# Placing small VectorE steps inside a matmul round, and pairing the context products of a two-layer graph network kernel

## The chip, the cores and the metric

The kernel runs on one core of one Trainium2 chip. The metric is device time in microseconds (us), from the first to the last instruction of the slowest core; here there is only one core. Three runs of the kernel before took 2916.56, 2917.6 and 2920.24 us, so the median is 2917.6 us. Engines are named as in the profile: PE (TensorE matmuls), PEld (TensorE weight loads), DVE (VectorE), ACT (ScalarE), POOL (GpSimd) and SP (SyncE, which here only issues transfers).

## The reference, cut to what matters

128 graphs with 64 nodes of 768 features pass through two layers; everything is fp32.

```
# layer 0, for each graph: h is 64 x 768, adj is 64 x 64
p    = softmax(h h^T / sqrt(768));  d = p * adj;  attn = d / (sum(d) + 1e-10)
ctx  = upper(attn) @ (h Wl^T + bl) + diag(attn) * (h Ws^T + bs) + lower(attn) @ (h Wr^T + br)
x    = layernorm(h + relu(layernorm(ctx) * gamma + beta))
# layer 1: 12 heads of 64 features
q, k, v = x Wq + bq, x Wk + bk, x Wv + bv
s    = q k^T / 8 + beta * adj, set to -9e15 where adj is 0
out  = layernorm(x + softmax(s) @ v)
```

The changed lines belong to layer 0: to the two products with Wl and Wr (the left and the right sides) and to the products of the attention matrix with them (the context).

## The kernel before, in words

**Blocks.** The 8192 tokens are cut into 16 blocks of 512 tokens (`NBLK`), each of four token tiles of 128 (`T`). In the steady state the loop `for n in range(NBLK)` works on layer 1 of block n and on layer 0 of block m = n + 1 at once, stage by stage: first the left and right sides of block m, then the self part of m, then the values of block n (with the context of m tucked in), then the query and key products of n for three groups of heads.

**Fast matrix products.** Large products use a seven-product scheme in place of eight (a Strassen-like scheme; `ORDER`, `ORDER2`). `seven` runs it on one level. `nested` (lines 425 to 501) runs it on two levels for the left and right sides of blocks 3 to 15: seven outer rounds i in the order 7, 1, 2, 6, 5, 4, 3, and in each of them seven inner products j. The inner products of two rounds are interleaved: after products 6, 5, 7 of round i come products 1 and 2 of the next round, and then 4 and 3 of round i. Below, 7(2) means inner product 7 of outer round 2. Products 1, 6, 7 and 4 of a round accumulate in one PSUM tile, X; product 2 writes a tile Y, and products 5 and 3 another. After products 1, 2, 6, 7, 4 and 3 the sum so far is read out of PSUM, plus a partner, into SBUF: this is an eviction (`middle`, `final`, `taken`, lines 439 to 458). Round 7 evicts most of X with ACT, the others evict with DVE at line 443. The next product that adds to the same PSUM tile has to come behind the eviction that reads it.

**Steps.** All other small work is kept in three queues, `first`, `urgent` and `lazy`, and a little of it is handed out by `step` behind each product (lines 137 to 156). An ordinary step lets DVE do one piece; a light step (`light=True`) issues no plain DVE piece and only takes pieces of other kinds, such as an ACT piece or a gap. In `sub` (lines 460 to 486) the call `step(len(done) > 8, j in (5, 1, 4))` makes the steps behind inner products 5, 1 and 4 light. So DVE pieces come behind 6, 7, 2 and 3. During the two-level stage these pieces are:

- of the layer-1 scores of an earlier block: an addition of the mask (line 860), a maximum (861), a subtraction (862), then 16 exponentials on ACT (853) and two transposes on DVE (857);
- of two weighted sums (`weighted`): four pieces each, a reciprocal (890) and four multiply-adds (894), which read PSUM tiles of the pool `ps_mm`.

**Context.** `context0` (lines 664 to 736) multiplies, for each of the four token tiles t, the transposed attention matrix with the left and right sides: four matmuls on 64 columns of the array each, into two PSUM tiles of `ps_mm` (a pool of four), behind them two DVE multiply-adds (line 684) and one ACT sum (687). These four `part`s are hung between the products of `values`, at places 1, 3, 5 and 7 of its 14 products; the steps that need all four sums come at place 9. In block 0 all four parts run in a row.

**Order.** Under `tc.manual_schedule()` the instructions of each engine stand in the order in which the code issues them. SP fetches the weights of the two-level stage (`wlr`, 63 pieces of 192 KB for each block, line 634) and all other weights into one pool of 19 buffers (`wst`).

Of the kernel before, what the change touches and what calls it, by code (L numbers as in the profile page):

```python
# [11 lines left out]
F32 = mybir.dt.float32  # L12
AF = mybir.ActivationFunctionType
ALU = mybir.AluOpType
# [3 lines left out]
P = 128  # L18
B, L, D = 128, 64, 768
# [3 lines left out]
HALF = D // 2  # L23
# [28 lines left out]
def gnn_two_layers(ctx: ExitStack, tc, x, adj, wl, bl, ws, bs, wr, br, gamma, beta,  # L52
                   wq, bq, wk, bk, wv, bv, abeta, out):
    nc = tc.nc
# [14 lines left out]
    ps_mm = ctx.enter_context(tc.tile_pool(name="ps_mm", bufs=4, space=PSUM))  # L69
# [51 lines left out]
    def later(key, *fs, queue=lazy):  # L121
        queue.extend((key, f) if callable(f) else (key, *f) for f in fs)
# [14 lines left out]
    def step(act_free=True, light=False):  # L137
        with tc.issue_after(recent["u"].ins) if recent.get("bound") else ExitStack():
            of_queues(act_free, light)
# [18 lines left out]
    def freed():  # L158

        while first:  # L160
            first.popleft()[1]()
# [12 lines left out]
    start = ExitStack()  # L174
# [250 lines left out]
    def nested(width, sums, load, multiply, view, C, bias0, bias1, hooks):  # L425

        X, Y, U, F, W = {}, {}, {}, {}, {}  # L430
        c11, c12, c21, c22 = C[0, 0], C[0, 1], C[1, 0], C[1, 1]
        out = {7: c22, 1: c21, 2: c11, 6: c21, 5: c12, 4: c21, 3: c12}
        old = {2: c21, 6: c21, 5: c21, 4: c21, 3: c12}
        done = []

        def part(i, q):
            return bias0(q[1]) if i == 1 else old[i][q] if i in old else None

        def taken(i, q, ps, dst, add):
            if add is None:  # L440
                nc.scalar.copy(dst, view(ps))
            else:
                nc.vector.tensor_tensor(dst, view(ps), add, ALU.add)  # L443

        def middle(i, q, ps, k):
            u = tmp.tile([P, HALF], F32, tag="u1" if k == 2 else "u0", name="u_deep")
            U[i, k] = view(u)
            taken(i, q, ps, U[i, k], part(i, q))
            if i == 5:
                nc.gpsimd.tensor_tensor(c21[q], c21[q], c22[q], ALU.add)  # L450

        def final(i, q, ps, add):
            taken(i, q, ps, out[i][q], add)
            if i == 5:
                if q == (1, 0):
                    nc.gpsimd.tensor_tensor(c21[q], c21[q], c22[q], ALU.add)
                nc.gpsimd.tensor_tensor(c12[q], c12[q], bias1(q[1]), ALU.add)
                nc.gpsimd.tensor_tensor(c22[q], c22[q], c12[q], ALU.add)

        def sub(i, j):  # L460
            for place in range(28):
                if place * 49 // 28 == len(done):
                    for f in hooks.get(place, ()):
                        f()
            done.append((i, j))
            if j == 1:
                X[i] = ps_st.tile([P, 512], F32, tag="X", name="ps_X")
            if j in (2, 5):
                Y[i] = ps_st.tile([P, 512], F32, tag="Y", name="ps_Y")
            ps = (X if j in (1, 6, 7, 4) else Y)[i][:, 0:width]  # L470
            multiply(F[i], W[i], j, ps)
            if j == 1:
                middle(i, (0, 0), ps, 1)
            elif j == 2:
                final(i, (0, 0), ps, U[i, 1])
            elif j == 6:
                middle(i, (0, 1), ps, 2)
            elif j == 7:
                middle(i, (1, 1), ps, 3)
                final(i, (1, 1), Y[i][:, 0:width], U[i, 3])  # L480
            elif j == 4:
                final(i, (1, 0), ps, part(i, (1, 0)))
            elif j == 3:
                final(i, (0, 1), ps, U[i, 2])

            step(len(done) > 8, j in (5, 1, 4))

        F[ORDER2[0]], W[ORDER2[0]] = sums(ORDER2[0]), load(ORDER2[0])
        sub(ORDER2[0], 1)
        sub(ORDER2[0], 2)  # L490
        for k, i in enumerate(ORDER2):
            after = ORDER2[k + 1] if k + 1 < len(ORDER2) else None
            if after:
                F[after], W[after] = sums(after), load(after)
            for j in (6, 5, 7):
                sub(i, j)
            if after:
                sub(after, 1)
                sub(after, 2)
            for j in (4, 3):  # L500
                sub(i, j)
# [162 lines left out]
    def context0(n):  # L664


        blk = blocks[n]
        xa, o, dg = blk["xa"], blk["x"], blk["dg"]
        by_act = n > 0
        if by_act:  # L670
            total, nm, var, std, rstd = (st.tile([P, T], F32, tag=f"c{k}", name=f"c{k}") for k in range(5))

        def unused():
            return l1s_p.tile([P, T * 4 * L], F32, tag="s", name="unused")[:, 0:D]

        def part(t):
            freed()
            for h in range(2):
                cols = slice(h * HALF, (h + 1) * HALF)
                ps = ps_mm.tile([P, 512], F32, tag="mm", name="ps_ctx")  # L680
                for g in range(2):
                    nc.tensor.matmul(ps[g * L : (g + 1) * L, 0:HALF], lhsT=blk["aT"][:, t, g * L : (g + 1) * L],  # L682
                                     rhs=blk["lr"][t][:, g, cols], start=True, stop=True)
                nc.vector.scalar_tensor_tensor(o[t][:, cols], o[t][:, cols], dg[:, t : t + 1], ps[:, 0:HALF],  # L684
                                               ALU.mult, ALU.add)
            if by_act:
                nc.scalar.activation(unused(), o[t], AF.Identity, accum_out=total[:, t : t + 1])  # L687
            elif t == T - 1:
                rest(moments(key, o, 1e-12))

        key = ("o", n)

        def squares():
            nc.vector.tensor_scalar(nm, total, -1.0 / D, None, ALU.mult)
            for t in range(T):
                nc.scalar.activation(unused(), o[t], AF.Square, bias=nm[:, t : t + 1], accum_out=var[:, t : t + 1])

        def roots():
            nc.vector.tensor_scalar(std, var, 1.0 / D, 1e-12, ALU.mult, ALU.add)
            nc.scalar.activation(std, std, AF.Sqrt)  # L700

        def inverse():
            nc.vector.reciprocal(rstd, std)
            rest([(nm[:, t : t + 1], rstd[:, t : t + 1]) for t in range(T)])

        def affine(t, mean, rstd):
            nc.vector.scalar_tensor_tensor(o[t], o[t], mean, affine_of["gamma"], ALU.add if by_act else ALU.subtract,
                                           ALU.mult)

        def affine2(t, mean, rstd):  # L710
            nc.vector.scalar_tensor_tensor(o[t], o[t], rstd, affine_of["beta"], ALU.mult, ALU.add)

        def residual(t):
            nc.vector.scalar_tensor_tensor(o[t], o[t], 0.0, xa[t], ALU.max, ALU.add)

        squared = 0 < n < NBLK - 1
        blk["x_d"] = x_d = tc.dram_tile([NTOK, D], F32, name=f"x1d_{n}") if squared else None

        def norm(t, mean, rstd):
            nc.vector.tensor_scalar(o[t], o[t], mean, rstd, ALU.subtract, ALU.mult)  # L720

        def stored():
            settle(key)
            for t in range(T):
                nc.gpsimd.dma_start(out=x_d[t * P : (t + 1) * P, :], in_=o[t])

        blk["stored"] = stored

        def rest(factors):
            for t, mr in enumerate(factors):  # L730
                fs = partial(affine, t, *mr), partial(affine2, t, *mr), partial(residual, t)
                later(key, *(fs if by_act else (fs[0], lambda fs=fs: (fs[1](), fs[2]()))))
            fs = [partial(norm, t, *mr) for t, mr in enumerate(moments(key, o, 1e-5))]
            later(key, *(fs if by_act else (lambda: (fs[0](), fs[1]()), lambda: (fs[2](), fs[3]()))))

        return [partial(part, t) for t in range(T)], (squares, roots, inverse)


# [283 lines left out]
    for n in range(NBLK):  # L1022
        m, p = n + 1, n - 1
        left, right, own, val = {}, {}, {}, {}
        qk = [{}, {}, {}]

        def at(hooks, place, f, *args):
            hooks.setdefault(place, []).append(partial(f, *args))
# [27 lines left out]
        if not last:  # L1056
            if n > 0:
# [9 lines left out]
                when, place = (left, 10) if n > 1 else (right, 2)  # L1067
# [45 lines left out]
                        at(own, 1 + t, f)  # L1113
                self_part(m, None, own)
            tiles, normal = context0(m)
            for t, f in enumerate(tiles):
                at(val, 1 + 2 * t, f)
            for hooks, place, f in ((val, 9, normal[0]), (val, 13, normal[1]), (qk[0], 1, normal[2])):
                at(hooks, place, f)
            if m + 1 < NBLK:  # L1120
# [163 lines left out]
```

## Time and profile before

| what | value |
|---|---|
| median of three runs | 2917.6 us |
| span of the profiled execution | 2916.3 us |
| median less that span | 1.3 us |
| PE busy | 2872.5 us, 98% of the span |
| DVE, ACT, POOL busy | 68%, 38%, 25% |
| granted TensorE clock, mean | 0.998 |
| PE instructions | 17578 (each fp32 matmul shows as two) |

The profile's busy time of PE counts the modelled end of each matmul, so that a short stall partly hides in it; stalls are read better from the distance between two starts. In the stages spoken of here an undisturbed instruction on 128 x 384 elements starts 0.3225 us after the one before it (24 of them take 7.74 us in the chain of waits), so that a product of one matmul takes 0.645 us (1, 6, 7) and one of two takes 1.29 us (2, 5, 4, 3).

In a timeline each line gives the start in us, the duration in us, the engine, the source line, the operation, what is written and read, the shapes and the number of merged instructions; the square bracket at its end is the idle time of the engine ahead of it and what ended it.

### The profile page before, as it was taken

The numbers are of one execution on the slowest core, as the hardware profiler recorded it, in microseconds if no ns is written. First come the engines' busy times: TensorE is split into PE (matmuls) and PEld (weight loads), VectorE is DVE, ScalarE is ACT, GpSimd is POOL, SyncE is SP. The second block draws the span as 40 slices with busy tenths as digits, with TensorE's granted clock in tenths as the row PEclk, the third lists the DMA queues.
The fourth block names the chain that finished last, engine by engine and source line by source line (L and its number), as shares of the span: only waits on it lengthen the run. The fifth ranks groups of instructions, "written<-read, shape, count | busy, mean of one in ns | idle before, by whom it ended". The sixth has DMA issues, their size and how long they took to land.

```text
span 2916.3 us, 49872 instructions
## 1 busy us (share of the span) xinstructions
PE 2872.5 (98%) x17578; PEld 1932.9 (66%) x17578; DVE 1974.3 (68%) x3973; ACT 1122.4 (38%) x2107; POOL 732.4 (25%) x879
## 2 busy tenths in 40 slices
PE   9999999999999999999999999999999999999997
PEld 5658567585665857658576675766757567585685
DVE  6678777676676766757667576766767667676655
ACT  0004224354243443434444344443434524344255
POOL 3133123213142140412405123051230512314110
PEclk9999999999999999999999999999999999999999
DMA  9788877859677595775958669486684956849443
GB/s 340 222 274 275 253 219 200 243 145 286 154 213 234 157 278 148 222 226 167 269 146 244 197 181 268 136 272 173 186 260 138 284 162 196 247 140 289 138 127 99
DMA packets 440662, 613.18 MB, mean 210 GB/s; under 512 B 53584, under 2 KB 416720, under 8 KB 440416
## 3 DMA queue, kind: packets, MB, share of 16 engines
q1 hardware_dynamic: 362960, 495.93, 56.1%
q10 hardware_dynamic: 60848, 44.05, 8.0%
q0 software_dynamic: 16608, 70.01, 6.7%
q8 instruction: 143, 2.34, 0.3%
q14 instruction: 103, 0.84, 0.1%
HBM read 539.43 MB, written 77.27 MB: 211 GB/s over the span
## 4 chain that ended last, share of the span: by engine, by line
PE 96%; POOL 2%; issue 1%; DVE 1%; ACT 0%; DMA 0%; POOLq 0%; SPq 0%; ACTq 0%
PE ps_X L389 38%; PE ps_Y L389 28%; PE ps_Y L643 11%; PE ps_X L643 10%; PE ps_ctx L682 3%; PE sc L833 2%; PE ps_y L884 2%; PE u L532 2%; POOL q L342 1%; POOL q L341 0%; PE ps_x L291 0%; POOL q L343 0%; ACT eT L853 0%; DMA xa<-in_x_dram 0%; DVE u_deep L443 0%
## 5 line engine op out<-in xcount | busy, mean ns | idle before, releaser
L389 PE MATMUL ps_X<-xT,wqk 128*128 128x256 f32 x1728 | 391.9, 380 | 0.6 <-ACT uqk L801 0.6
L853 ACT ACTIVATE eT<-s 32x256 f32<-32x256 f32 x768 | 317.8, 414 | 171.6 <-DVE s L862 161.6
L389 PEld LDWEIGHTS ps_X<-xT,wqk 128*128 128x128 f32 x1728 | 327.0, 190 | 52.9 <-ACT k L807 4.6
L322 POOL TENSOR_TENSOR S<-hT 128x768 f32<-128x768 f32 x16 | 29.0, 1810 | 1133.6 <-PE ps_Y L389 1102.1
L389 PE MATMUL ps_Y<-S,wqk 128*128 128x256 f32 x1152 | 264.3, 379 | 0.0
L687 ACT ACTIVATE unused<-o 128x768 f32<-128x768 f32 x60 | 50.6, 844 | 499.6 <-DVE o L684 305.3
L389 PEld LDWEIGHTS ps_Y<-S,wqk 128*128 128x128 f32 x1152 | 218.9, 190 | 29.8
L443 DVE TENSOR_TENSOR lr<-ps_Y,u_deep 128x384 f32<-128x384 f32 x273 | 151.6, 555 | 96.8 <-PE ps_Y L643 71.0
L643 PE MATMUL ps_Y<-wlr,q 128*128 128x384 f32 x546 | 208.5, 491 | 0.0
L801 ACT ACTIVATE uqk<-ps_X,bq 128x256 f32<-128x256 f32 x144 | 68.3, 474 | 333.1 <-PE ps_X L389 332.4
L389 PE MATMUL ps_X<-wv,xT 128*128 128x384 f32 x576 | 195.5, 489 | 0.0
L389 PE MATMUL ps_X<-ws,hT 128*128 128x384 f32 x540 | 179.2, 486 | 0.0
L809 DVE TENSOR_TENSOR q<-ps_Y,uqk 128x256 f32<-128x256 f32 x144 | 61.0, 424 | 169.7 <-PE ps_Y L389 97.4
L643 PE MATMUL ps_X<-wlr,q 128*128 128x384 f32 x364 | 152.0, 499 | 16.8 <-POOL q L342 5.9
L389 PEld LDWEIGHTS ps_X<-wv,xT 128*128 128x128 f32 x576 | 108.0, 190 | 80.4 <-issue 8.4
L894 DVE SCALAR_TENSOR_TENSOR o<-ps_y,rz,o 128x64 f32<-128x64 f32 x720 | 154.7, 277 | 6.4
L443 DVE TENSOR_TENSOR u_deep<-ps_X,lr 128x384 f32<-128x384 f32 x195 | 107.3, 551 | 68.3 <-PE ps_X L643 66.6
L389 PEld LDWEIGHTS ps_X<-ws,hT 128*128 128x128 f32 x540 | 102.5, 190 | 71.4
L643 PEld LDWEIGHTS ps_Y<-wlr,q 128*128 128x128 f32 x546 | 101.6, 190 | 67.2
L420 DVE TENSOR_TENSOR u<-ps_X,bv 128x384 f32<-128x384 f32 x96 | 53.4, 556 | 130.9 <-PE ps_X L389 130.9
L389 PE MATMUL ps_X<-S,wqk 128*128 128x256 f32 x576 | 138.3, 385 | 0.0
L389 PE MATMUL ps_Y<-xT,wqk 128*128 128x256 f32 x576 | 135.6, 385 | 0.0
(258 smaller groups left out, 5467.2 us busy)
## 6 DMA issues: line engine op xcount, KB each, us to landing
wlr<-lr_d SPq DMA_DIRECT2D x819, 192.0 KB, 3.4
wqk<-qk_d SPq DMA_DIRECT2D x672, 192.0 KB, 2.4
wv<-d_v SPq DMA_DIRECT2D x192, 192.0 KB, 2.9
ws<-d_s SPq DMA_DIRECT2D x180, 192.0 KB, 5.7
wv<-in_L_gnn_Wv_dram SPq DMA_DIRECT2D x144, 192.0 KB, 4.1
ws<-in_L_gnn_W_self_dram SPq DMA_DIRECT2D x135, 192.0 KB, 5.4
xa<-in_x_dram SPq DMA_DIRECT2D x64, 384.0 KB, 4.9
sq<-in_x_dram ACTq DMA_DIRECT2D x56, 384.0 KB, 7.8
```

The costliest lines, as they stand in the source:

```text
L389: nc.tensor.matmul(ps, lhsT=a, rhs=b, start=(c == 0 and i in (1, 2, 5)), stop=(c == len(fs) - 1), skip_group_check=True)
L420: recent["u"] = evicted[nm] = nc.vector.tensor_tensor(u, ps, bias[nm][:, b * HALF : (b + 1) * HALF], ALU.add)
L443: nc.vector.tensor_tensor(dst, view(ps), add, ALU.add)
L532: nc.tensor.matmul(u[g * L : (g + 1) * L, t, :], lhsT=xT[:, c, tok], rhs=xT[:, c, tok], start=(c == 0), stop=(c == KC - 1))
L643: nc.tensor.matmul(ps, lhsT=a, rhs=b, start=(k == 0 and j in (1, 2, 5)), stop=(k == len(fs) - 1), skip_group_check=True)
L682: nc.tensor.matmul(ps[g * L : (g + 1) * L, 0:HALF], lhsT=blk["aT"][:, t, g * L : (g + 1) * L], rhs=blk["lr"][t][:, g, cols], start=True, s ...
L801: nc.scalar.activation(u, ps, AF.Identity, bias=bias["qk"[j]][:, c : c + 1])
L809: nc.vector.tensor_tensor(dst, ps, part, ALU.add)
L833: nc.tensor.matmul(sc[r][g * L : (g + 1) * L, t, c, :], lhsT=q[rows, c, tok], rhs=k[rows, c, tok], start=True, stop=True)
L853: nc.scalar.activation(e[to[0], :, to[1]], pairs[rows, :, cols], AF.Exp)
L884: nc.tensor.matmul(y[r, h][cols, t, c, :], lhsT=eT[rows, 2 * h + t, c, cols], rhs=v[rows, 2 * h + t, g, hg + c * HC, :], start=True, stop= ...
L894: nc.vector.scalar_tensor_tensor(res[:, r, c, hg, :], ps[:, t, c, 0:HD], rz[:, t, c : c + 1], res[:, r, c, hg, :], ALU.mult, ALU.add)
```

## The change

There are two edits. First, in the two-level stage the steps behind inner products 5, 1 and 3 are light, in place of 5, 1 and 4: the fourth DVE piece of a round comes behind product 4 and no longer behind product 3. Second, the context products of two token tiles are issued as one group, ahead of the first of their two `part`s, into all four tiles of the pool; and the four parts move from places 1, 3, 5, 7 to places 1, 2, 5, 6.

```diff
-            step(len(done) > 8, j in (5, 1, 4))
+            step(len(done) > 8, j in (5, 1, 3))
...
+        banks = {}
+
+        def multiplied(ts):
+            freed()
+            for t in ts:
+                for h in range(2):
+                    ps = banks[t, h] = ps_mm.tile([P, 512], F32, tag="mm", name="ps_ctx")
+                    for g in range(2):
+                        nc.tensor.matmul(ps[g * L : (g + 1) * L, 0:HALF], lhsT=blk["aT"][:, t, g * L : (g + 1) * L],
+                                         rhs=blk["lr"][t][:, g, h * HALF : (h + 1) * HALF], start=True, stop=True)
+
         def part(t):
-            freed()
+            if t % 2 == 0:
+                multiplied((t, t + 1))
             for h in range(2):
                 cols = slice(h * HALF, (h + 1) * HALF)
-                ps = ps_mm.tile([P, 512], F32, tag="mm", name="ps_ctx")
-                for g in range(2):
-                    nc.tensor.matmul(ps[g * L : (g + 1) * L, 0:HALF], lhsT=blk["aT"][:, t, g * L : (g + 1) * L],
-                                     rhs=blk["lr"][t][:, g, cols], start=True, stop=True)
-                nc.vector.scalar_tensor_tensor(o[t][:, cols], o[t][:, cols], dg[:, t : t + 1], ps[:, 0:HALF],
-                                               ALU.mult, ALU.add)
+                nc.vector.scalar_tensor_tensor(o[t][:, cols], o[t][:, cols], dg[:, t : t + 1],
+                                               banks.pop((t, h))[:, 0:HALF], ALU.mult, ALU.add)
...
             tiles, normal = context0(m)
-            for t, f in enumerate(tiles):
-                at(val, 1 + 2 * t, f)
+            for place, f in zip((1, 2, 5, 6), tiles):
+                at(val, place, f)
```

## The prediction

> **What bounds the kernel now.** I read the page first, then PE's waits, then the timelines of one two-level stage (block 5, 652 to 709 us) and of the values stage behind it. The page says that PE is the bound everywhere:
>
> ```profile
> PE 2872.5 (98%) x17578; PEld 1932.9 (66%) x17578; DVE 1974.3 (68%) x3973; ACT 1122.4 (38%) x2107; POOL 732.4 (25%) x879
> PE 96%; POOL 2%; issue 1%; DVE 1%; ACT 0%; DMA 0%; POOLq 0%; SPq 0%; ACTq 0%
> ```
>
> So only what makes PE faster counts. PE's waits (us in total, times, longest) show where it loses time: line 643, the two-level stage.
>
> ```profile
> PE ps_X L643 <- POOL q L342: 5.9, 13, 0.5
> PE ps_X L643 <- issue: 5.6, 29, 0.2
> PE ps_X L643 <- POOL q L344: 3.1, 13, 0.2
> ```
>
> The counts are 13, 13 and 29: the same few waits in each of 13 stages. The releasers named are not the true ones, as the timeline shows. PE first, from 3(7)'s end to 1(2):
>
> ```profile
> 664.16 0.81 PE L643 MATMUL ps_X<-wlr,q 128*128 128x384 f32 x2
> 664.81 0.81 PE L643 MATMUL ps_Y<-wlr,q 128*128 128x384 f32 x2
> 665.46 0.81 PE L643 MATMUL ps_Y<-wlr,hT 128*128 128x384 f32 x2
> 666.47 0.88 PE L643 MATMUL ps_X<-wlr,q 128*128 128x384 f32 x2 [0.21 <-issue]
> 667.19 0.81 PE L643 MATMUL ps_X<-wlr,hT 128*128 128x384 f32 x2
> ```
>
> These are 6(1), 5(1) in two lines, 7(1) and 1(2). 7(1) should start at 664.81 + 1.29 = 666.10 and starts at 666.47: 0.37 us late. DVE at the same time:
>
> ```profile
> 664.37 0.56 DVE L443 TENSOR_TENSOR lr<-ps_Y,u_deep 128x384 f32<-128x384 f32 x1 [1.35 <-PE ps_Y L643]
> 664.84 0.17 DVE L890 RECIPROCAL rz<-ps_y 128x4 f32<-128x4 f32 x1
> 665.05 0.86 DVE L894 SCALAR_TENSOR_TENSOR o<-ps_y,rz,o 128x64 f32<-128x64 f32 x4
> 665.82 0.55 DVE L443 TENSOR_TENSOR u_deep<-ps_X,bias_lr 128x384 f32<-128x384 f32 x1
> ```
>
> The first line evicts 3(7); then comes the small piece behind product 3, 0.98 us; only then the eviction of 6(1), which could have begun at 664.81 + 0.2. Product 7 adds to the tile that this eviction reads, and starts 0.65 us after its start. That is the true releaser. Around 7(2) the piece is the subtraction:
>
> ```profile
> 672.48 1.21 DVE L862 TENSOR_TENSOR s<-s,mx 128x1024 f32<-128x1024 f32 x1
> 673.61 0.55 DVE L443 TENSOR_TENSOR u_deep<-ps_X,lr 128x384 f32<-128x384 f32 x1
> ...
> 674.26 0.88 PE L643 MATMUL ps_X<-wlr,q 128*128 128x384 f32 x2 [0.46 <-POOL q L342]
> ```
>
> (673.61 to 674.26 is 0.65 again.) In the values stage, the second place where PE loses:
>
> ```profile
> 736.16 2.10 PE L389 MATMUL ps_X<-wv,xT 128*128 128x384 f32 x6
> 738.19 1.51 PE L682 MATMUL ps_ctx<-lr,aT 128*64 128x384 f32 x8
> 739.63 2.20 PE L389 MATMUL ps_X<-wv,xT 128*128 128x384 f32 x6
> 741.67 2.10 PE L389 MATMUL ps_Y<-wv,xT 128*128 128x384 f32 x6
> 743.70 1.51 PE L682 MATMUL ps_ctx<-lr,aT 128*64 128x384 f32 x8
> ```
>
> From one context group to the next is 743.70 - 738.19 = 5.51 us. The twelve ordinary instructions are worth 12 x 0.3225 = 3.87. Block 0, where all context products stand in one group, takes 5.31 us for 32 instructions, and 5.31 - 1.44 (the group of 8 here) over the 24 more is 0.161 each, so eight are worth 1.29. The remaining 0.35 us belongs to each group: some 0.10 ahead of it, 0.15 in it, 0.10 in the first matmul behind it.
>
> **What the Trainium skill says.** PSUM — Partial Sum Buffer, section "PSUM bank collisions raise a hardware error": two engines must not be on one bank's quadrant at once and software has to guard it by semaphore; so 7 cannot overlap the eviction of 6. The trace agrees: 0.65 us from start to start, twice. The same page, "Engine vs sequencer instructions": VectorE's queue is strictly first in, first out, so an eviction cannot pass a small piece; the DVE lines above agree. TensorEngine Tiling (Array Packing), "Key Properties": changing the tiling mode drains the array. The 0.35 us on every change from 128 to 64 columns and back agrees in kind. Perfetto Trace Analysis, "Optimization Strategy": the same gap repeating on the engine that should be saturated may mean too few buffers; here the trace shows late evictions instead.
>
> **Part 1, the moved step.** It removes no instruction; it moves one DVE piece per round ahead of the eviction of 3. No transfer of SP or POOL changes its place. On ACT, the exponentials now stand ahead of all four `sq<-x1d` loads instead of around the first.
>
> What it removes: the piece behind product 3 delays four products 7 of each stage. From starts: 7(1) 0.37; 7(2) 674.26 against 672.35 + 1.29 = 0.62; 7(6), behind a transpose, 681.83 against 680.14 + 1.29 = 0.40; 7(5) 690.66 against 689.00 + 1.29 = 0.37. The sum is 1.76. Each also stretches the product behind the stall from 0.645 to 0.72 (666.47 to 667.19), four times 0.075 = 0.30. Together 2.06 us a stage, 26.8 us in 13 stages. Other waits (6(7) on ACT, 4(3) on DVE) stay.
>
> What comes back: I walk DVE through the new order with these rows: eviction 0.47 to the next start, 0.6 to 0.65 where the next needs its result, weighted piece 0.98, eviction possible 0.2 after its product's end.
> - Round 7. The queue's contents shift too: the subtraction (1.13) now comes behind 4(7), from 663.1 to 664.2, while DVE used to wait (idle 1.35). Eviction of 3(7) at 664.37 as before, of 6(1) at 665.01, so 7(1) starts at 666.10: no stall.
> - Round 1. The four weighted pieces come behind 6, 7, 2(2) and 4(1). 7(1) evicted at 666.95 and 667.55, piece to 669.0, evictions of 1(2) and 2(2) at 669.0 and 669.64, piece to 671.09, eviction of 4(1) to 671.56, piece to 672.54, of 3(1) to 673.01, of 6(2) at 673.01. 7(2) can start at 673.66, and 5(2) ends at 673.20: a stall of 0.46, plus 0.075. DVE has a backlog here, and no place would hide it.
> - Round 2. The transposes come behind 6(2) and 7(2), nothing behind 4(2): no stall at 7(6).
> - Round 6. A piece behind 2(5) and one behind 4(6). With the PE times of this walk: 4(6) evicted 686.27 to 686.74, piece to 687.72, 3(6) to 688.19, 6(5) at 688.19, so 7(5) is free at 688.84, ahead of 689.14: no stall, by 0.30.
>
> So 0.53 us a stage remains and 2.06 - 0.53 = 1.53 goes: 19.9 us in 13 stages. The moved piece costs nothing otherwise because the eviction of 3 has no early reader on PE: the next product that adds to that tile is a full round away. Bounds: 0.53 more (26.8) if no backlog stall is left; half of 19.9, 10 us, if 7(5) and one more go on stalling.
>
> **Part 2, the pairs.** Matmuls, adds and sums are the same in number. In 15 blocks, four groups become two, and 2 x 0.35 = 0.70 us goes: 10.5 us. The moved adds (two of 0.6 us for tiles 1 and 3) come earlier, into a DVE that idles about 1.4 us ahead of nearly each eviction here; without that cover a late eviction would have to exceed a whole 1.94 us product. The group needs four `ps_mm` tiles at once: their last readers are the attention transpose's (706.84, a stage earlier) and, at place 5, the adds of tiles 0 and 1, issued three products (5.8 us) before. Bounds: 0, if changing tiles inside a group costs what the mode change does, against which block 0 speaks; 12.
>
> **Sum.** 19.9 + 10.5 = 30.4 us off the span, 2916.3 to 2885.9; the median runs stand 1.3 above the span: **2887.2 us**, 1.04% less.
>
> **Rivals.**
> 1. DVE's backlog only moves: product 7 goes on stalling in every loaded round, and part 1 brings 0 to 10 us. For it: round 1 shows exactly that. Against: before the evictions of 3(7), 3(2) and 3(6) DVE idles 1.35, 0.73 and 0.57 us, which is the room that the piece takes. It gives about 2897 to 2907 us.
> 2. No backlog stall is left, because DVE's pitch is a little shorter than in my walk (0.1 us in each of five places): 2880 us. Four pieces and seven evictions in one round (3.9 + 7 x 0.47 + 0.4 = 7.6 us against 7.1 of PE) speak against it.
> 3. Slower: on ACT the `sq<-x1d` loads are issued earlier, from about 671 us in place of 675, and could collide with `wlr`. A weight buffer comes round after 19 x 56.9 / 63 = 17 us; a `wlr` piece lands in 3.4 us (median), 8.6 at most. PE waits only from 17 us on; at 20 us, a loss of 2.8 a stage, the kernel is slower: about 2924 us. The DMA share argues against it: 0.73 from 666 to 673 us, 1.10 from 680 to 690, so the loads move to where there is room.
> 4. The edit does nothing: the order of the changed program's instructions does show the pieces ahead of 3's eviction and the groups of 16 on PE, so this is excluded but for 2% within 0.2%.
>
> **How the numbers follow.** My forecast 0.66, rival 1 0.17, rival 2 0.11, rival 3 0.04, no difference 0.02. Range 2878 to 2901: the forecast with its bounds, rival 2 and the better half of rival 1. About 0.2% (5.8 us) is what a measurement of this kernel can tell from no change: faster 0.94, same 0.02, slower 0.04.
>
> **What would show it.** PE's waits at line 643 fall from some 19.6 us to about 9; a single stall of about 0.46 a stage stays, at 7(2), besides those of 6(7) and 4(3); the stage of block 5 takes 55.4 us in place of 56.9. Context groups show 16 instructions in about 2.73 us, two for each block. Wrong would be: waits at 7(1), 7(6) or 7(5); a group of 16 that takes 2.9; PE waiting on `wlr`.

## The result, and the profile after

The changed kernel takes 2889.86 us (median of 4 runs, 2888.21 to 2891.61) against 2917.08 us for the kernel before (4 runs): a ratio of 0.9906, 95% interval 0.9893 to 0.9919. That is 27.2 us less; 30.4 were forecast (2887.2 us, range 2878 to 2901).

The page of the changed kernel, PE still the bound:

```profile
PE 2852.7 (99%) x17578; PEld 1940.3 (67%) x17578; DVE 1971.5 (68%) x3973; ACT 1121.9 (39%) x2107; POOL 717.5 (25%) x879
```

PE's waits at line 643 (us in total, times, longest). There were 78 before; 39 are left, three in each of the 13 stages, and their sum fell from 19.5 to 12.0 us:

```profile
PE ps_X L643 <- POOL q L344: 6.9, 13, 0.9
PE ps_X L643 <- DVE u_deep L443: 2.8, 13, 0.2
PE ps_X L643 <- issue: 2.3, 13, 0.2
```

The second and third are those of 4(3) and 6(7), which the change does not touch. The first is the one of 7(2).

The timelines are of the stage that the prediction calls that of block 5; the name is kept here, though it is the second of the 13 stages, so that in the count from 3 to 15 its block is number 4. DVE (start, duration, line, operation, what is written and read), from 4(7) to the eviction of 6(1): the subtraction, line 870 now, fills what was an idle gap, and the two evictions follow without a piece between them:

```profile
658.81 1.23 DVE L870 TENSOR_TENSOR s<-s,mx 128x1024 f32<-128x1024 f32 x1
660.13 0.56 DVE L443 TENSOR_TENSOR lr<-ps_Y,u_deep 128x384 f32<-128x384 f32 x1
660.77 0.56 DVE L443 TENSOR_TENSOR u_deep<-ps_X,bias_lr 128x384 f32<-128x384 f32 x1
```

PE at the same time: 5(1) in two lines, then 7(1) without a bracket, 1.29 us after the start of 5(1):

```profile
660.57 0.81 PE L643 MATMUL ps_Y<-wlr,q 128*128 128x384 f32 x2
661.22 0.81 PE L643 MATMUL ps_Y<-wlr,hT 128*128 128x384 f32 x2
661.86 0.81 PE L643 MATMUL ps_X<-wlr,q 128*128 128x384 f32 x2
```

DVE in the loaded round: the eviction of 4(1), the fourth weighted piece, the eviction of 3(1), that of 6(2):

```profile
666.87 0.55 DVE L443 TENSOR_TENSOR lr<-ps_X,bias_lr 128x384 f32<-128x384 f32 x1
667.33 0.17 DVE L898 RECIPROCAL rz<-ps_y 128x4 f32<-128x4 f32 x1
667.54 0.86 DVE L902 SCALAR_TENSOR_TENSOR o<-ps_y,rz,o 128x64 f32<-128x64 f32 x4
668.31 0.55 DVE L443 TENSOR_TENSOR lr<-ps_Y,u_deep 128x384 f32<-128x384 f32 x1
668.97 0.56 DVE L443 TENSOR_TENSOR u_deep<-ps_X,lr 128x384 f32<-128x384 f32 x1
```

and PE, where 7(2) is the one product 7 that still waits:

```profile
667.67 0.81 PE L643 MATMUL ps_Y<-wlr,q 128*128 128x384 f32 x2
668.31 0.81 PE L643 MATMUL ps_Y<-wlr,hT 128*128 128x384 f32 x2
669.62 0.88 PE L643 MATMUL ps_X<-wlr,q 128*128 128x384 f32 x2 [0.50 <-POOL q L344]
```

7(2) should start at 667.67 + 1.29 = 668.96; it is 0.66 us late, and 669.62 is again 0.65 after the start of the eviction that it needs (668.97). Last, the context on PE:

```profile
730.60 2.10 PE L389 MATMUL ps_X<-wv,xT 128*128 128x384 f32 x6
732.63 2.80 PE L684 MATMUL ps_ctx<-lr,aT 128*64 128x384 f32 x16
735.36 2.20 PE L389 MATMUL ps_X<-wv,xT 128*128 128x384 f32 x6
```

Sixteen instructions in 2.73 us (732.63 to 735.36), one entry and one exit for two tiles.

**Where the time went.** The two-level stage of block 5 took 56.93 us from its first product to the first of the self part (652.14 to 709.07); it now takes 55.61 (647.90 to 703.51): 1.32 us less. The 13 such stages together took 740.2 us and take 723.3, which is 16.9 less; 13 x 1.32 would be 17.2, but in one stage, which begins at 2243.3 us, 7(2) waits 0.87 us in place of 0.50 and the stage takes 55.98. The values stage took 33.65 us (736.16 to 769.81) and takes 32.95 (730.60 to 763.55): 0.70 us, in 15 blocks 10.5. These 27.4 us, and 0.7 us of PE's wait for the first load of `xa` (7.1 and 6.4 us in all, which varies from run to run), make 28.1 of the 28.2 us between the two spans (2916.3 and 2888.1); between the medians it is 27.2.

### The profile page after: what moved, and what is told of

Read it like the earlier page. It is cut to its first block, busy times and chain, and to the rows that moved or that the text cites. A ratio compares the mean times of both kernels' runs of the same rounds, so it can differ in the third digit from the quotient of the medians.

```text
span 2888.1 us, 49913 instructions
## 1 busy us (share of the span) xinstructions
PE 2852.7 (99%) x17578; PEld 1940.3 (67%) x17578; DVE 1971.5 (68%) x3973; ACT 1121.9 (39%) x2107; POOL 717.5 (25%) x879
## 4 chain that ended last, share of the span: by engine, by line
PE 97%; POOL 1%; issue 1%; DVE 1%; ACT 0%; DMA 0%; POOLq 0%; SPq 0%; ACTq 0%
PE ps_X L389 38%; PE ps_Y L389 28%; PE ps_Y L643 12%; PE ps_X L643 10%; PE ps_ctx L684 3%; PE sc L841 2%; PE ps_y L892 2%; PE u L532 2%; PE ps_x L291 0%; POOL q L343 0%; ACT eT L861 0%; DVE u_deep L443 0%; DMA xa<-in_x_dram 0%; POOL q L341 0%; POOL q L342 0%
## 5 line engine op out<-in xcount | busy, mean ns | idle before, releaser
L695 ACT ACTIVATE unused<-o 128x768 f32<-128x768 f32 x60 | 50.6, 843 | 478.7 <-DVE o L692 218.7
L948 ACT ACTIVATE unused<-o 128x768 f32<-128x768 f32 x60 | 50.6, 843 | 266.6 <-DVE o L902 165.6
```

## The experiments

The theory: DVE works through its queue in order, and a small piece ahead of the eviction of product 6 makes product 7 late; a change between 128 and 64 columns costs PE 0.35 us a group. The rivals are named with each run. All medians are compared with the kernel before, measured on the same chip (2917.16 us in the first four runs, 2917.49 in the last three). "Both edits" is the changed kernel, 2889.86 us where the kernel before took 2917.08.

**1. The moved step alone**

```diff
-            step(len(done) > 8, j in (5, 1, 4))
+            step(len(done) > 8, j in (5, 1, 3))
```

> Only the moved step, context groups as before. Theory (late evictions of product 6 behind a VectorE piece): the stage of block 5 takes 55.6 us as with both edits, against 56.9, so 13 x 1.32 = 17 us less than before: about 2900 us. Rival (the stage's gain comes from the changed context groups or from their earlier sums): no more than 3 us less, 2914 us or above.

Measured: 2899.91 us, ratio 0.9943 (0.993 to 0.9955). The stage of block 5 takes 55.60 us (650.02 to 705.62), as with both edits. The gain of this stage is that of the moved step and of nothing else.

**2. The pairs alone**

```diff
-            step(len(done) > 8, j in (5, 1, 3))
+            step(len(done) > 8, j in (5, 1, 4))
```

(an edit to the changed kernel)

> Only the paired context groups, steps as before. Theory (each entry into and exit from 64 columns costs 0.35 us in all): 15 x 0.70 = 10.5 us less than before, about 2906.6 us, with the waits at line 643 as before (19.5 us). Rival (the cost belongs to the matmuls or to changing PSUM tiles, not to the group): 0 to 3 us less, 2914 us or above.

Measured: 2907.73 us, ratio 0.9966 (0.9953 to 0.9978), so 9.4 us less. The values stage takes 32.95 us, as with both edits, and so brings 10.5 us in 15 blocks. The two parts add up: 17.25 and 9.4 are 26.7, both together gave 27.2. PE's waits at line 643 are those of before, 19.9 us in all:

```profile
PE ps_X L643 <- issue: 8.3, 39, 0.8
PE ps_X L643 <- POOL q L342: 5.5, 12, 0.5
...
PE ps_X L643 <- POOL q L344: 3.1, 13, 0.2
PE ps_X L643 <- DVE u_deep L443: 2.8, 13, 0.2
...
PE ps_X L643 <- POOL q L343: 0.2, 1, 0.2
```

**3. No piece behind 4 in the loaded round**

```diff
-            step(len(done) > 8, j in (5, 1, 3))
+            step(len(done) > 8, j in (5, 1, 3) or (i, j) == (1, 4))
```

> Both edits, and the step behind 4(1) is light too, so that the last weighted piece of the loaded round goes behind 6(2) and the transposes one step later. Theory (the stall left at 7(2) is VectorE's backlog of that round: 0.66 us and 0.075 behind it): the stall goes, 13 x 0.735 = 9.6 us less than with both edits, about 2880 us. Rival 1 (GpSimd's sums, which the profile names as releaser): the wait stays, 2889 us. Rival 2 (the transposes, now later, make the second weighted sum wait): a new PE wait at its line, 2885 us or above.

Measured: 2881.51 us, ratio 0.9878 (0.9863 to 0.9893); 8.35 us less than with both edits, faster than both kernels. The wait that the profile had put down to `POOL q L344` is gone, although no instruction of GpSimd was touched, and no new wait appears at line 892. DVE around 3(1), 6(2) and the piece that is now behind them:

```profile
666.61 0.55 DVE L443 TENSOR_TENSOR lr<-ps_Y,u_deep 128x384 f32<-128x384 f32 x1
667.26 0.56 DVE L443 TENSOR_TENSOR u_deep<-ps_X,lr 128x384 f32<-128x384 f32 x1
667.74 0.17 DVE L898 RECIPROCAL rz<-ps_y 128x4 f32<-128x4 f32 x1
```

PE: 7(2), the last line, starts 1.29 us after 5(2) and without a bracket.

```profile
666.94 0.81 PE L643 MATMUL ps_Y<-wlr,q 128*128 128x384 f32 x2
667.59 0.81 PE L643 MATMUL ps_Y<-wlr,hT 128*128 128x384 f32 x2
668.23 0.81 PE L643 MATMUL ps_X<-wlr,q 128*128 128x384 f32 x2
```

So the releaser named in a wait was not the true one, and the stall that was left was DVE's backlog. Of the 9.6 us expected, 1.2 did not come. The stages do bring it: that of block 5 takes 54.87 us (647.18 to 702.05) in place of 55.61. But in two blocks PE now waits for the self part's weights (three short waits, 0.8 us in all), and the self part behind takes 27.83 and 28.05 us there in place of 27.09, which is 1.7 us more. No such wait is seen with both edits alone.

**4. Context products in half-tile groups**

```diff
-            if t % 2 == 0:
-                multiplied((t, t + 1))
-            for h in range(2):
+            for h in halves:
+                multiplied(t, h)
...
-            for place, f in zip((1, 2, 5, 6), tiles):
-                at(val, place, f)
+            for t, f in enumerate(tiles):
+                for h in range(2):
+                    at(val, 1 + 2 * t + h, partial(f, halves=(h,)))
```

(`multiplied` issues one half of one tile, and the ACT sum follows the second half.)

> The moved step kept; context products in eight groups for each block, half a token tile each, in place of two. Theory (0.35 us for each group): six groups more in 15 blocks, 6 x 0.35 x 15 = 31.5 us more than with both edits, about 2921 us. Rival (no cost of a group, but of matmuls): unchanged, 2890 us. In between if part of the 0.35 us is the first pair of matmuls on a new tile, which goes with the tiles: 2900 to 2910 us.

Measured: 2921.08 us, ratio to before 1.0013 (1.0007 to 1.002); 31.2 us above both edits. PE's timeline:

```profile
738.96 0.87 PE L682 MATMUL ps_ctx<-lr,aT 128*64 128x384 f32 x4
739.76 2.20 PE L389 MATMUL ps_X<-wv,xT 128*128 128x384 f32 x6
741.89 0.87 PE L682 MATMUL ps_ctx<-lr,aT 128*64 128x384 f32 x4
```

From group to group 2.93 us, less six times 0.3225 and four times 0.161: 0.35. The values stage takes 35.04 us in place of 32.95: 2.09 us for six groups more, again 0.35 each. The cost is of the group, whether it has 4, 8 or 16 instructions. The Trainium skill (TensorEngine Tiling (Array Packing), section "Key Properties") says that a change of the tiling mode drains the array; the runs show what such a change costs here, not which part of it is the drain.

**5. Taking away the dependence of 6(2) on 3(1)**

```diff
-            return bias0(q[1]) if i == 1 else old[i][q] if i in old else None
+            return bias0(q[1]) if i == 1 or (i, q) == (2, (0, 1)) else old[i][q] if i in old else None
```

> Both edits; the eviction of 6(2) adds the bias in place of the sum that the eviction of 3(1) has just written, so one addend of the second round is another value and the left and right sides come out different. Theory (the part of the stall at 7(2) that the walk missed is VectorE waiting for its own result): from the eviction of 3(1) to that of 6(2) 0.47 us in place of 0.66, the stall 0.46 in place of 0.66, 13 x 0.2 = 2.6 us less than with both edits, about 2887.3 us. Rival (the 0.2 us comes from elsewhere, the PSUM reads or GpSimd): the distance stays at 0.66, 2889.9 us.

Measured: 2887.28 us, ratio 0.9896 (0.9883 to 0.991). DVE's evictions of 3(1) and 6(2), now 0.47 us apart:

```profile
669.28 0.55 DVE L443 TENSOR_TENSOR lr<-ps_Y,u_deep 128x384 f32<-128x384 f32 x1
669.75 0.55 DVE L443 TENSOR_TENSOR u_deep<-ps_X,bias_lr 128x384 f32<-128x384 f32 x1
```

PE, 5(2)'s second half and 7(2):

```profile
669.28 0.81 PE L643 MATMUL ps_Y<-wlr,hT 128*128 128x384 f32 x2
670.40 0.88 PE L643 MATMUL ps_X<-wlr,q 128*128 128x384 f32 x2 [0.31 <-POOL q L344]
```

7(2) is late by 670.40 - 669.28 - 0.645 = 0.475 us in place of 0.66. The medians' difference of 2.6 us alone would not be clear of their scatter (2885.91 to 2888.8 and 2888.21 to 2891.61); the wait in the profile, 4.0 us in 13 stages in place of 6.9, is. Ten of the 13 stages take 55.41 or 55.42 us in place of 55.61. The other three take 0.25 to 0.5 us longer than these, two of them with a short wait of PE for a piece of `wlr` (0.5 us in all), so that the medians come out at 2.6 us apart partly by luck.

**6. No piece behind 4 in any round**

```diff
-            step(len(done) > 8, j in (5, 1, 3))
+            step(len(done) > 8, j in (5, 1, 3, 4))
```

> Both edits, and the step behind product 4 is light in every round, so that a round hands out three pieces only. Theory (late evictions are not all: what the pieces feed must be ready in time): no stall at any 7, 9.6 us less; but the subtraction comes a round later, behind 7(2), the exponentials mix with the sq loads on ScalarE, and the second weighted sum waits for its transposes, 2 to 6 us in each of 13 stages: 2906 to 2958 us, with a PE wait at line 892. Rival (only what stands ahead of the eviction of 6 counts): about 2880 us.

Measured: 2936.45 us, ratio 1.0064 (1.005 to 1.0077). No product 7 waits any more, and the kernel is slower than before. PE's waits name the new one:

```profile
PE ps_y L892 <- DVE eT L865: 38.5, 14, 2.9
```

The subtraction comes at 672.91 us, behind 7(2), the exponentials run on ACT until 680.97, and the transposes, which the second weighted sum needs, start at 681.00. PE's timeline from 7(6) on:

```profile
678.10 0.81 PE L643 MATMUL ps_X<-wlr,q 128*128 128x384 f32 x2
681.77 1.80 PE L892 MATMUL ps_y<-v,eT 64*64 64x65 f32 x64 [2.86 <-DVE eT L865]
683.49 1.65 PE L643 MATMUL ps_X<-wlr,S 128*128 128x384 f32 x2
684.93 1.73 PE L643 MATMUL ps_Y<-wlr,S 128*128 128x384 f32 x4
```

The wait itself is 2.9 us, but what follows is slow too: 1.72 us for the weighted sum, where both edits took 1.10 (677.53 to 678.63), 1.44 for 1(5) against 0.75, 1.57 for 2(5) against 1.28, together 1.60 us more. The busy times of short stretches, with the granted TensorE clock ahead of the last two columns (DMA share, GB/s), say why:

```profile
681.70:682.70 1.00, 0.93 (x43) 0.93 (x46) 0.61 (x2) 0.00 (x0) 0.00 (x0) 0.69 1.01 213
682.70:683.70 1.00, 1.00 (x33) 0.88 (x28) 0.00 (x0) 0.00 (x0) 0.00 (x0) 0.50 1.13 185
683.70:684.70 1.00, 1.00 (x2) 0.63 (x3) 0.00 (x0) 0.00 (x0) 0.00 (x0) 0.50 1.13 160
684.70:685.70 1.00, 1.00 (x3) 0.50 (x2) 0.52 (x1) 0.00 (x0) 0.00 (x0) 0.61 0.80 118
685.70:686.70 1.00, 1.00 (x4) 0.60 (x4) 0.04 (x1) 0.00 (x0) 0.82 (x1) 1.00 0.61 145
```

The sum of 2.9 + 1.6, less 0.735 for the stall that went, is 3.8 us, and the stage of block 5 takes 59.40 us in place of 55.61. In the first of the 13 stages the wait is as long (2.86 us) but the clock stays at 1.00, and the stage takes 57.94 us. All 13 together take 769.5 us against 723.3 with both edits, 46.2 more; between the medians it is 46.6.

**7. The first eviction of a stage by DVE**

```diff
-            if add is None:
+            if add is None and (i, q) == (7, (0, 0)):
+                nc.vector.tensor_copy(dst, view(ps))
+            elif add is None:
                 nc.scalar.copy(dst, view(ps))
```

(an edit to the kernel of run 3)

> As the run with no piece behind 4(1), and the eviction of 1(7) done by VectorE in place of ScalarE. Theory (the wait at 6(7) is that eviction standing behind four exponentials on ScalarE, 0.34 us and 0.075 behind it): that wait goes, 13 x 0.41 = 5.3 us less, about 2876 us. Rival (VectorE is no earlier, since it has transposes and the eviction of 2(7) there): 2881 us or above.

Measured: 2892.01 us, ratio 0.9912 (0.9898 to 0.9925), 10.5 us slower than run 3: the rival was right. DVE's timeline shows the copy behind a transpose that had itself waited for the same exponentials:

```profile
649.59 0.71 DVE L867 STREAM_TRANSPOSE eT<-eT 128x512 f32<-128x512 f32 x1 [1.10 <-ACT eT L863]
650.23 0.52 DVE L441 COPY u_deep<-ps_X 128x384 f32<-128x384 f32 x1
```

So the wait at 6(7) grew from 0.18 to 0.89 us of idle time, in 13 stages 9.2 us. Most of the rest is one block in which PE also waits for weights, 1.05 us for `wlr` and 1.15 for the self part's. The cause of the wait at 6(7), exponentials ahead of an eviction, is the same on either engine, and moving the eviction alone does not help.

## Why the prediction was right, and which term was mis-sized

**What bounds it.** Right: the waits that the profile put down to GpSimd and to issue were late evictions on DVE. Run 3 took the last of them away by moving DVE pieces only, and run 1 put the gain of the stage on the step.

**Part 1, what is removed.** The four stalls at 7(1), 7(2), 7(6) and 7(5) were priced at 2.06 us a stage. 7(1), 7(6) and 7(5) start without a wait now, as the walk said. The price was right too: in run 3, where none of the four is left, the stage of block 5 takes 54.87 us, 2.06 less than 56.93.

**Part 1, what comes back.** The mis-sized term is "evictions of 3(1) and of 6(2) at 672.54 and 673.01" in round 1: the walk put the next eviction 0.47 us later, but 6(2) adds what the eviction of 3(1) has just written, so that the distance is 0.66. The stall at 7(2) is 0.66 us in place of 0.46, in 13 stages 2.6 us. With that term the sum is 30.4 - 2.6 = 27.8 us, against 28.2 between the spans and 27.2 between the medians. The walk had used the longer distance "where the next needs its result" inside a round, between the evictions of 1 and 2 or of 7's two tiles, and had not looked for it across rounds. Run 5 shows it by taking the dependence away. It eats into round 6 too: 6(5)'s eviction starts at 684.42, 0.65 after that of 3(6) at 683.77, so 7(5) is free at 685.07 and starts at 685.18, a margin of 0.11 in place of the 0.30 predicted. Apart from this the walk held: shifted by the 4.23 us that PE had gained until then, the evictions of 3(7) and 6(1) and the end of the fourth weighted piece stand where it put them, to 0.02 us.

**Part 2.** Right, in size too: 0.70 us in the values stage of block 5 and 2.73 us for a group of 16. Run 2 measured 9.4 us of the 10.5 by itself, run 4 the price of a group with the opposite sign. No wait for the four PSUM tiles appeared in PE's waits.

**The rivals.** The moved backlog (rival 1) is true of one round only. No stall left (rival 2) would have needed a shorter pitch; the pitch was longer. The loads of `sq` (rival 3) do start earlier, though not as the prediction had it: the first is issued at 665.09 us, still ahead of four exponentials and not behind all sixteen, the others from 671.63. SP's waits for these loads at line 634 rise from 11.3 to 68.4 us in all (71.8 in run 1 and 13.5 in run 2, so this comes with the moved step), and a piece of `wlr` lands in 3.8 us (median; 10.1 at most) in place of 3.4 and 8.6. No matmul waits for one with both edits. But the 17 us from which PE was to wait are not the limit: in run 5 no piece takes longer than 10.2 us to land, and PE waits for `wlr` in two stages; in run 7 no piece takes longer than 9.5, and PE waits 1.05 us once. So this rival was nearer than the prediction thought, and that it cost nothing here is partly luck. That the edit does nothing (rival 4) is excluded.

**What was to be seen.** The waits at line 643 were to fall to about 9 us; they fell to 12.0, 2.6 of the difference of 3.0 being the mis-sized term, 13 x 0.2, and 0.4 the one longer wait at 7(2).

## What to carry to other kernels

When a matmul adds to a PSUM tile that another engine has to read first, count the products between them: small work on the reading engine belongs ahead of a read that nothing waits for soon, not ahead of the one with the shortest deadline, and one piece fewer in the fullest round can be worth more than the better place. Follow each moved piece to what it feeds: taking it out of the way by one round made a later product wait 2.9 us. Issue small matmuls of another array shape in as few groups as their PSUM tiles allow.

## What the runs showed of the hardware that was not expected

In run 6 PE was idle for some 2.86 us once in each of the 13 stages. In 12 of them the granted clock then fell: in the stage of block 5 it was 0.69, 0.50, 0.50 and 0.61 in the next four stretches of 1 us, and 1.00 again some 4 us after work began. These four stretches lack 1.70 us of full clock, and the products in them took 1.60 us more. In the first stage the clock stayed at 1.00 behind the same wait (in the second line it stands ahead of the last two columns):

```profile
502.17 1.29 PE L892 MATMUL ps_y<-v,eT 64*64 64x65 f32 x64 [2.86 <-DVE eT L865]
502.85:503.85 1.00, 1.00 (x37) 0.80 (x35) 0.00 (x0) 0.00 (x0) 0.00 (x0) 1.00 1.20 141
```

So the length of the wait alone does not decide it; what does is left open. With both edits the clock stays at 1.00 in the same stretch of block 5, although the DMA share is as high there (1.02 to 1.18), and the waits of 0.89 us in run 7 lowered it in no stage.

On DVE, the eviction of 6(2) follows that of 3(1) in 0.47 us when it does not need its result (run 5) and in 0.66 us when it does; between the two evictions of 7(1), of which the second reads what the first wrote, it is 0.59 us (662.71 to 663.30 with both edits). An instruction placed between two such evictions fills up to 0.19 us for nothing, as the piece behind product 3 did in the kernel before.
